# Two graph layers on one core: attention scores with keys on partitions, their sums by a matrix of ones, and a fixed round of stages on TensorE

## The chip, the cores and the metric

The kernel runs on one core of one Trainium2 chip. The metric is the device time of one execution in microseconds. Three executions of the kernel before gave 3097.95, 3098.14 and 3100.08 us; the median is 3098.14 us.

Engines: TensorE (PE, with its weight loads as a row of their own, PEld), VectorE (DVE), ScalarE (ACT), GpSimd (POOL) and SyncE (SP, which issues DMAs here). Matmuls write PSUM, which has eight banks of 2 KB per partition; GpSimd works on SBUF only here. All data is float32.

## The reference

`x` has 64 graphs of 256 nodes with 512 features; `adj` is one 256x256 matrix of zeros and ones, the same for all graphs, symmetric, with ones on its diagonal. Layer 0 is masked attention with 8 heads of 64, a residual and a layer norm; layer 1 is a graph attention layer with one score per pair of nodes, a residual and a layer norm.

```python
q, k, v = x @ Wq + bq, x @ Wk + bk, x @ Wv + bv          # split in 8 heads of 64
scores = q k^T / 8 + (1 - adj) * -1e9
attn = softmax(scores)                                    # over the keys
x = layernorm(x + (attn v) @ Wo + bo)
h = x @ W
s1, s2 = h @ a[:512], h @ a[512:]
e = leaky_relu(s1[:, None] + s2[None, :], 0.2) * adj
x = layernorm(x + elu(softmax(e) h + beta * h))
```

## The kernel before

One graph is called a batch here (b = 0 to 63). Tiles have 128 partitions: a batch's 256 nodes are two blocks t, its 512 features four blocks c.

**A batch's stages.** `tr_x` (line 423) transposes x on TensorE into `xT`, and GpSimd adds the folded biases `res_sb` onto x (428). `project` (301) multiplies by a 512x512 weight with seven block products instead of eight (the sums of blocks come from `weight_sums`, once, and from `token_sums`, four GpSimd subtractions per operand, line 292). A product is made of matmuls at line 315 (result with features on partitions: q, k) or 319 (nodes on partitions: v, o, u). Its results are copied out of PSUM by ACT (lines 442, 445) or DVE (542), and further parts are added by DVE (451, 542). In the projection o both are DVE additions onto x (542). Product 6 accumulates onto the bank of product 1 (`ps_chain`), so it has to wait until product 1's copy has been read; the order on TensorE is products 1, 5, 2, 6, 3, 4, 7.

`scores(t, g)` (467): for a block t of 128 queries and four heads, four matmuls (474) with queries on partitions and 256 keys along the free axis; DVE adds the mask and finds the row minimum of the negated scores (481); ACT takes the exponential with that as bias and sums the row (485); DVE inverts the sums (489); GpSimd multiplies the probabilities by them (490). `flip(h)` (495) transposes a head's probabilities on TensorE (501), so that keys are on partitions, and ACT or DVE copies them out (505, 507). `mix(g)` (511) multiplies them with v (519), and DVE copies the result, `oT` (524). The projection o follows, then `norm` (385).

The second layer: two weighted sums over the features on DVE (555), a small transpose (564, "logits" in the change), the leaky score matrix (569 to 582, with GpSimd's product with `adj` in 573), its transpose (591, "attention" in the change), the mixing of x (`spread`, 605), the projection u, the exponential and two DVE additions (625 to 628), `norm`, and the store (631).

**The order of the work.** Nothing is issued directly: each step is given to `Plan.op` (64) with an engine, a duration, what it reads and writes, and, on TensorE, a mode ("rows" for scores, "columns" for mix, else none). `Plan.place` (91) is a list scheduler: at each step it takes, on the engine that can start first, the ready operation with the earliest start, and the oldest in the program among equals; a change of mode on TensorE costs 250 ns in its books. `slots` (181) limits the live tiles by kind: 8 PSUM banks, 10 tiles of 8 KB and so on. The result is one fixed order of instructions for each engine, all 64 batches unrolled; on the chip every engine works through its list in order and waits by semaphores. Small constants are loaded by the GpSimd queue at the start, the weights by ACT's queue, x and the output by SP's.

Of the kernel before, what the change touches and what calls it, by code (L numbers as in the profile page):

```python
# [9 lines left out]
F32 = mybir.dt.float32  # L10
AF = mybir.ActivationFunctionType
# [8 lines left out]
NEG = -1000000000.0  # L20

# [23 lines left out]
class Plan:  # L45
# [6 lines left out]

    LAG = {"PE": 260.0, "DVE": 70.0, "ACT": 70.0, "POOL": 90.0, "SP": 2200.0, "LD": 2200.0}
    SWITCH = 250.0

    def __init__(self, slots):
        self.slots = dict(slots)
        self.ops = []

# [4 lines left out]
    def op(self, engine, ns, fn, reads=(), writes=(), mode=None, claims=()):  # L64
# [24 lines left out]
        self.ops.append((engine, ns, fn, deps, bufs, mode))  # L89

    def place(self):
# [3 lines left out]
        for n, o in enumerate(ops):  # L95
            need[n] = len(o[3])
            for d in o[3]:
                users[d].append(n)
        end = [0.0] * len(ops)
# [9 lines left out]
        while len(order) < len(ops):  # L109
            best = None  # L110
            for e, cand in ready.items():
                pick = None
                for n in cand:
# [15 lines left out]
                    cost = self.SWITCH if e == "PE" and m != mode else 0.0  # L129
                    key = (max(start + cost, now[e] + 60.0), n)  # L130
# [7 lines left out]
            if e == "PE" and m != mode:  # L138
                start += self.SWITCH
                mode = m  # L140
            for b in bufs:
# [27 lines left out]
def gnn_two_layers(ctx: ExitStack, tc: tile.TileContext, x, adj, Wq, bq, Wk, bk, Wv, bv, Wo, bo, W, a, beta, out):  # L169
# [9 lines left out]
    psum = ctx.enter_context(tc.tile_pool(name="psum", bufs=1, space=PSUM))  # L179

    slots = {"x": 4, "full": 10, "p": 6, "half": 15, "xS": 2, "st": 90, "ps": 8}
# [10 lines left out]
    sb_pool, ps_pool = Pool(big), Pool(psum)  # L192
    plan = Plan(slots)
    A = slice(None)
# [10 lines left out]
    def once(shape, name):  # L205
# [3 lines left out]
        return sb(name, shape, name)  # L209
# [13 lines left out]
    def weight(w, name):  # L223
        w_sb = once([C, D], name)
        plan.op("LD", 4500, lambda: nc.scalar.dma_start(w_sb[A], w.rearrange("(c p) f -> p c f", p=P)), [], [w_sb])
        return w_sb

# [19 lines left out]
    bo_sb = on_all(bo, 0, D, "bo_sb")  # L247
# [3 lines left out]
    a_sb = [on_all(a, i * D, D, f"a{i}_sb") for i in range(2)]  # L251

    mask_sb = once([NT, N], "mask_sb")

    def mask():
        nc.vector.tensor_scalar(mask_sb[A], adj_sb, -1.0, 1.0, ALU.mult, ALU.add)
        nc.vector.tensor_scalar(mask_sb[A], mask_sb[A], NEG * HD ** 0.5, None, ALU.mult)

    plan.op("DVE", 900, mask, [], [mask_sb])


# [83 lines left out]
    def residual_bias():  # L345
        acc = ps([D], "ps_b")
# [7 lines left out]
        plan.op("DVE", 690, lambda: nc.vector.tensor_add(res_sb[A], acc[A], bo_sb), [acc], [res_sb])  # L354
# [6 lines left out]
    def second_layer_constants():  # L361
# [4 lines left out]
        for i in range(2):  # L366
            col = st(C, "col")
            for c in range(C):
                junk = sb("half", [D], "junk")
                plan.op("DVE", 780, lambda c=c, i=i, junk=junk, col=col: nc.vector.scalar_tensor_tensor(  # L370
# [296 lines left out]
```

## Time and profile before

| what | number |
|---|---|
| median of three executions | 3098.14 us |
| profiled execution, its own time | 3099.26 us |
| its span, first to last instruction | 3097.50 us |
| granted TensorE clock over the span | 0.994 |
| PE busy | 3033.8 us |
| PE work per batch away from the ends, start of a mix to the start of the next | 46.99 us |
| DVE, ACT, POOL busy in such a stretch of 46.99 us | 34.10, 25.18, 23.30 us |
| scores, mix, spread and all flips of one batch on PE | 3.65, 3.60, 3.45 and 3.50 us |

"Busy" is the time in which an engine has an instruction in execution. The chain of waits is the list of work that ended last, traced back from the last instruction: an engine with nearly all of it sets the time. A group of instructions carries the line of the kernel, the engine, and the tiles by name, as output<-input. PE's pieces in that chain follow each other without overlap, so their lengths can be added.

### The profile page before, as it was taken

To read this page: it belongs to the slowest core of one execution; us is meant where nothing else is said; L and a number is where in the kernel's file an instruction comes from. 1 tells how busy PE (TensorE), PEld (TensorE's weight loads), DVE (VectorE), ACT (ScalarE), POOL (GpSimd) and SP (SyncE) were. 2 spreads that over 40 slices of the span, in tenths; PEclk is the share of its full clock that TensorE was granted. 3 is DMA by queue.
4 is the path that set the end of the run, shared out by engine and by line. 5 is a ranking of instruction groups with operands and counts; after the bars stand their busy time and mean duration, and the time that the engine had idled before them with its cause. 6 is when DMAs were issued, how large, how long until landed. Compare 5 with 4: busy or idle time off the path is not lost.

```text
span 3097.5 us, 56539 instructions
## 1 busy us (share of the span) xinstructions
PE 3033.8 (98%) x20624; PEld 2673.7 (86%) x20624; DVE 2202.2 (71%) x6303; ACT 1614.5 (52%) x4737; POOL 1521.2 (49%) x1756
## 2 busy tenths in 40 slices
PE   8999999999999999999999999999999999999995
PEld 7778898898898888888988888988988889888884
DVE  4678667677677677676686676776776776766865
ACT  3455555455455555555555554554555555555552
POOL 6355445445445455454454454454554554544543
PEclk9999999999999999999999999999999999999998
DMA  3000000000000000000000000000000000000000
GB/s 109 1 28 28 28 15 28 22 22 28 18 25 28 15 28 28 15 28 28 15 28 28 15 28 21 22 28 18 25 28 15 28 28 15 28 28 15 28 15 14
DMA packets 39205, 77.03 MB, mean 25 GB/s; under 512 B 3344, under 2 KB 3344, under 8 KB 38928
## 3 DMA queue, kind: packets, MB, share of 16 engines
q1 hardware_dynamic: 35840, 67.12, 6.0%
q10 hardware_dynamic: 2640, 5.24, 0.5%
q8 instruction: 164, 2.69, 0.4%
q0 software_dynamic: 448, 1.06, 0.1%
q14 instruction: 113, 0.93, 0.1%
HBM read 39.85 MB, written 33.55 MB: 24 GB/s over the span
## 4 chain that ended last, share of the span: by engine, by line
PE 95%; DVE 2%; POOL 1%; issue 1%; ACT 0%; DMA 0%; SPq 0%; POOLq 0%; ACTq 0%; DVEq 0%
PE ps_chain L319 16%; PE ps_chain L315 11%; PE ps_pair L319 11%; PE ps_cross L319 10%; PE ps_cross L315 7%; PE ps_pair L315 7%; PE ps_sc L474 7%; PE ps_y L605 7%; PE ps_pv L519 7%; PE tr_p L501 7%; PE tr_x L423 2%; PE tr_a L591 1%; PE tr_s L564 0%; DMA x<-in_x_dram 0%; DVE junk L555 0%
## 5 line engine op out<-in xcount | busy, mean ns | idle before, releaser
L485 ACT ACTIVATE p<-p,nm 128x256 f32<-128x256 f32 x1024 | 506.3, 496 | 23.7 <-DVE nm L481 16.4
L490 POOL TENSOR_TENSOR p<-p,rc 128x1024 f32<-128x1024 f32 x256 | 484.3, 1892 | 51.6 <-DVE rc L489 50.3
L481 DVE CUSTOM_DVE_ANT_0 p<-ps_sc,mask_sb 128x256 f32<-128x256 f32 x1024 | 386.0, 413 | 4.6 <-PE ps_sc L474 4.6
L292 POOL TENSOR_TENSOR yS<-yT 128x256 f32<-128x256 f32 x128 | 93.7, 732 | 548.7 <-ACT yT L610 543.7
L392 POOL TENSOR_SCALAR rs<-mv 128x1 f32<-128x1 f32 x256 | 78.5, 306 | 565.5 <-DVE mv L389 565.5
L398 ACT ACTIVATE x<-x,nmr,rs 128x512 f32<-128x512 f32 x256 | 208.3, 814 | 248.0 <-DVE nmr L396 248.0
L501 PE MATMUL tr_p<-ident,p 128*128 128x128 f32 x2048 | 247.7, 274 | 6.1 <-POOL p L490 3.0
L474 PE MATMUL ps_sc<-kT,qT 64*128 64x256 f32 x2048 | 240.5, 383 | 1.9 <-DVE oT L524 1.6
L519 PE MATMUL ps_pv<-pT,v 128*64 128x256 f32 x2048 | 237.6, 384 | 4.4 <-DVE pT L507 2.3
L501 PEld LDWEIGHTS tr_p<-ident,p 128*128 128x128 f32 x2048 | 229.3, 142 | 9.3 <-issue 4.0
L396 DVE SCALAR_TENSOR_TENSOR nmr<-mv,rs 128x1 f32<-128x1 f32 x256 | 227.7, 889 | 13.3 <-POOL rs L393 2.3
L605 PE MATMUL ps_y<-attT,x 128*128 128x256 f32 x1024 | 233.7, 381 | 1.6 <-ACT attT L594 1.6
L474 PEld LDWEIGHTS ps_sc<-kT,qT 64*128 64x128 f32 x2048 | 193.3, 187 | 46.8 <-issue 23.4
L573 POOL TENSOR_TENSOR e<-e,adj_sb 128x512 f32<-128x512 f32 x64 | 81.4, 1271 | 293.5 <-DVE rc L489 275.0
L605 PEld LDWEIGHTS ps_y<-attT,x 128*128 128x128 f32 x1024 | 195.4, 191 | 29.7 <-ACT attT L594 2.6
L519 PEld LDWEIGHTS ps_pv<-pT,v 128*64 128x64 f32 x2048 | 141.6, 138 | 82.4 <-DVE x L628 9.7
L451 DVE TENSOR_TENSOR v<-ps_pair,v 128x256 f32<-128x256 f32 x64 | 27.2, 425 | 232.8 <-PE ps_pair L319 232.8
L485 ACT ACTIVATION_READ_ACCUMULATOR p<-p,nm 128x1 f32 x1024 | 192.1, 188 | 0.0
L388 DVE BATCH_NORM_STATS2 bn<-x 128x6 f32<-128x512 f32 x256 | 175.6, 686 | 6.6
L505 ACT COPY pT<-tr_p 128x512 f32<-128x512 f32 x256 | 148.8, 582 | 51.9 <-PE tr_p L501 45.5
L507 DVE COPY pT<-tr_p 128x512 f32<-128x512 f32 x256 | 169.8, 683 | 5.4 <-PE tr_p L501 5.3
L445 ACT ACTIVATE qT<-ps_chain,bq_sb 128x128 f32<-128x128 f32 x256 | 79.7, 361 | 180.0 <-PE ps_chain L315 180.0
(168 smaller groups left out, 7516.1 us busy)
## 6 DMA issues: line engine op xcount, KB each, us to landing
x<-in_x_dram SPq DMA_DIRECT2D x64, 512.0 KB, 3.6
out_dram<-x SPq DMA_DIRECT2D x128, 256.0 KB, 2.0
wq_sb<-in_L_gnn_Wq_dram ACTq DMA_DIRECT2D x1, 1024.0 KB, 10.0
wk_sb<-in_L_gnn_Wk_dram ACTq DMA_DIRECT2D x1, 1024.0 KB, 7.6
wv_sb<-in_L_gnn_Wv_dram ACTq DMA_DIRECT2D x1, 1024.0 KB, 5.8
wo_sb<-in_L_gnn_Wo_dram ACTq DMA_DIRECT2D x1, 1024.0 KB, 5.5
w_sb<-in_L_gnn_W_dram ACTq DMA_DIRECT2D x1, 1024.0 KB, 5.6
a_sb<-in_L_gnn_a_dram POOLq DMA_DIRECT2D x2, 256.0 KB, 8.5
```

The source lines that it names most:

```text
L315: nc.tensor.matmul(dst[:, f, :], l[:, c, blk(f)], r[:, c, :], start=start and f == 0 and c == 0, stop=c == 1, skip_group_check=True)
L319: nc.tensor.matmul(dst, r[:, c, :], l[:, c, :], start=start and c == 0, stop=c == 1, skip_group_check=True)
L388: plan.op("DVE", 690, lambda: nc.vector.bn_stats(bn[A], X[:, t, :]), [(X, (t, 0)), (X, (t, 1))], [bn])
L396: plan.op("DVE", 150, lambda: nc.vector.scalar_tensor_tensor(nm[A], mv[:, 0:1], -1.0, rs[A], op0=ALU.mult, op1=ALU.mult), [mv, rs], [nm])
L398: plan.op("ACT", 810, lambda: nc.scalar.activation(X[:, t, :], X[:, t, :], AF.Identity, bias=nm[A], scale=rs[A]), [nm, rs], [(X, (t, 0)), ...
L474: nc.tensor.matmul(acc[i % 2][:, i // 2, :], qT[r:r + HD, h // 2, blk(t)], kT[r:r + HD, h // 2, :], start=True, stop=True)
L481: plan.op("DVE", 420, lambda i=i: nc.vector.tensor_tensor_reduce(p[:, i, :], acc[i % 2][:, i // 2, :], mask_sb[:, t, :], -1.0 / HD ** 0.5, ...
L485: plan.op("ACT", 690, lambda i=i: nc.scalar.activation(p[:, i, :], p[:, i, :], AF.Exp, bias=nm[t][g][:, i:i + 1], scale=-1.0, accum_out=sm ...
L490: plan.op("POOL", 1900, lambda: nc.gpsimd.tensor_tensor(p[A], p[A], rc[A].unsqueeze(2).to_broadcast([P, 4, N]), ALU.mult), [rc, p], [p])
L501: nc.tensor.transpose(tr[:, k, blk(t)], pr[t][h // 4][:, h % 4, blk(k)], ident)
L519: nc.tensor.matmul(acc[s * HD:(s + 1) * HD, i, :], V[:, k, h * HD:(h + 1) * HD], pT[h][:, k, :], start=k == 0, stop=k == NT - 1)
L605: nc.tensor.matmul(acc[:, i, :], X[:, j, c * P:(c + 1) * P], attT[:, j, :], start=j == 0, stop=j == NT - 1)
```

## The change

In the first layer the scores are computed with keys on partitions: `kT` is the stationary operand and `qT` the moving one, one PSUM bank per head. ACT takes the exponential straight from PSUM with no maximum subtracted; DVE multiplies it by the transposed `adj` (made once on TensorE); the result is already what mix needs, so the flips and their copies are gone. GpSimd adds a head's two key blocks, and a matmul with a matrix of ones and zeros (`ones`, 32 columns, four results at partitions 0, 32, 64 and 96) sums over the partitions. DVE inverts the sums, SP writes one row per head to DRAM and reads it back onto 64 partitions each (`everywhere`), and DVE multiplies mix's result by it in place of the plain copy. ACT also sums the denominators and their inverses into `range_sb`.

TensorE's order is no longer the scheduler's choice: each TensorE step has a turn, made of a round and a place in `ROUND`. A round holds mix of batch r-1, scores of r, x of r+1, spread of r-2, o of r-1, u of r-2, v of r, logits of r-1, sums of r, q and k of r+1, attention of r-1. On the other engines, among operations that can start equally early, the one needed first by TensorE goes first. The slots change (x 5, tiles of 8 KB 9, of 2 KB 24).

At the end a test of `range_sb` decides whether a general version (maximum subtracted, queries on partitions, a loop over the batches) does all batches again. Two constants now come by ACT's queue when they are needed (`bo`, `a`).

```diff
+    LATER = 20
...
     def place(self):
...
+        turns = [n for _, n in sorted(self.turns, reverse=True)]
+        due = [None] * len(ops)
+        for i, n in enumerate(reversed(turns)):
+            due[n] = i
+        for n in reversed(range(len(ops))):
+            for u in users[n]:
+                if due[u] is not None and (due[n] is None or due[u] < due[n]):
+                    due[n] = due[u]
+        for n, o in enumerate(ops):
+            if due[n] is None:
+                due[n] = max((due[d] + (self.LATER if ops[d][0] == "PE" else 0) for d in o[3]), default=0)
         end = [0.0] * len(ops)
         base = [0.0] * len(ops)
...
                 pick = None
+                if e == "PE":
+                    cand = turns[-1:] if turns and turns[-1] in cand else []
...
                         continue
-                    cost = self.SWITCH if e == "PE" and m != mode else 0.0
-                    key = (max(start + cost, now[e] + 60.0), n)
+                    key = (max(start, now[e] + 60.0), due[n], n)
                     if pick is None or key < pick[0]:
...
             for b in bufs:
                 if not b.held:
...
-    slots = {"x": 4, "full": 10, "p": 6, "half": 15, "xS": 2, "st": 90, "ps": 8}
+    dram = ctx.enter_context(tc.tile_pool(name="dram", bufs=1, space=bass.MemoryType.DRAM))
+    slots = {"x": 5, "full": 9, "half": 24, "xS": 4, "st": 90, "ps": 8, "rows": 4}
...
-    mask_sb = once([NT, N], "mask_sb")
...
-    plan.op("DVE", 900, mask, [], [mask_sb])
+    ones = const.tile([P, 48], F32, name="ones")
+    nc.gpsimd.memset(ones, 0.0)
+    nc.gpsimd.memset(ones[:, 16:32], 1.0)
...
+            for k in range(NT):
+                for t in range(NT):
+                    nc.tensor.transpose(acc[:, k, blk(t)], adj_sb[:, t, blk(k)], ident)
+        plan.op("PE", 430, pe, [], [acc], claims=[adjT_sb])
+        plan.op("DVE", 690, lambda: nc.vector.tensor_copy(adjT_sb[A], acc[A]), [acc], [adjT_sb])
...
+        def turn(what):
+            later = {"x": -1, "q": -1, "k": -1, "scores": 0, "v": 0, "sums": 0, "mix": 1, "o": 1, "logits": 1,
+                     "attention": 1, "spread": 2, "u": 2}[what]
+            plan.turn = (n + later, ROUND.index(what))
+        plan.op("SP", 60, lambda: nc.sync.dma_start(X[A], x[at].rearrange("o (t p) d -> p (o t) d", p=P)), [],
                 [(X, (t, i)) for t in range(NT) for i in range(2)])
-        return X
...
-            acc = [ps([2, N], "ps_sc") for _ in range(2)]
-            def pe():
-                for i in range(4):
-                    h, r = 4 * g + i, (i % 2) * HD
-                    nc.tensor.matmul(acc[i % 2][:, i // 2, :], qT[r:r + HD, h // 2, blk(t)],
-                                     kT[r:r + HD, h // 2, :], start=True, stop=True)
-            plan.op("PE", 870, pe, [(qT, (g, t)), (kT, (g, 0)), (kT, (g, 1))], acc, mode="rows",
-                    claims=[pr[t][g], nm[t][g], sm[t][g]])
-            p = pr[t][g]
-            for i in range(4):
-                plan.op("DVE", 420, lambda i=i: nc.vector.tensor_tensor_reduce(
-                    p[:, i, :], acc[i % 2][:, i // 2, :], mask_sb[:, t, :], -1.0 / HD ** 0.5, 3.0e38, ALU.add,
-                    ALU.min, nm[t][g][:, i:i + 1]), [acc[i % 2], mask_sb], [(p, i), nm[t][g]])
-            for i in range(4):
-                plan.op("ACT", 690, lambda i=i: nc.scalar.activation(
-                    p[:, i, :], p[:, i, :], AF.Exp, bias=nm[t][g][:, i:i + 1], scale=-1.0,
-                    accum_out=sm[t][g][:, i:i + 1]), [(p, i), nm[t][g]], [(p, i), (sm[t][g], i)])
...
-            plan.op("POOL", 1900, lambda: nc.gpsimd.tensor_tensor(
-                p[A], p[A], rc[A].unsqueeze(2).to_broadcast([P, 4, N]), ALU.mult), [rc, p], [p])
...
-            plan.op("PE", 430, pe, [pr[t][h // 4] for t in range(NT)], [tr], claims=[pT[h]])
-            if h % 2:
-                plan.op("ACT", 580, lambda: nc.scalar.copy(pT[h][A], tr[A]), [tr], [pT[h]])
-            else:
-                plan.op("DVE", 690, lambda: nc.vector.tensor_copy(pT[h][A], tr[A]), [tr], [pT[h]])
...
+        def mixed(pT, g, onto, reads=()):
+            turn("mix")
...
-            plan.op("PE", 1740, pe, [(V, (g, 0)), (V, (g, 1))] + pT[4 * g:4 * g + 4], [acc], mode="columns",
-                    claims=[oT])
-            plan.op("DVE", 690, lambda: nc.vector.tensor_copy(oT[:, 2 * g:2 * g + 2, :], acc[A]), [acc], [(oT, g)])
+            plan.op("PE", 1740, pe, [(V, (g, 0)), (V, (g, 1))] + pT[4 * g:4 * g + 4] + list(reads), [acc],
+                    mode="columns", claims=[oT])
+            plan.op("DVE", 690, lambda: onto(acc), [acc] + list(reads), [(oT, g)])
+        def attention_by_keys():
+            pT = [sb("half", [NT, N], "pT") for h in range(H)]
+            both = [sb("half", [2, N], "both") for c in range(C)]
+            inv, everywhere = sb("half", [N], "inv"), sb("full", [C, N], "inv_all")
+            rows = Buf(dram_pool, "rows", [H, N], "rows")
+            def scores(g):
+                turn("scores")
+                acc = [ps([NT, N], "ps_sc") for _ in range(4)]
+                def pe():
+                    for i in range(0, 4, 2):
+                        for k in range(NT):
+                            for s in range(2):
+                                h, r = 4 * g + i + s, s * HD
+                                nc.tensor.matmul(acc[i + s][:, k, :], kT[r:r + HD, h // 2, blk(k)],
+                                                 qT[r:r + HD, h // 2, :], start=True, stop=True)
+                plan.op("PE", 1740, pe, [(m, (g, j)) for m in (qT, kT) for j in range(NT)], acc, mode="rows",
+                        claims=pT[4 * g:4 * g + 4] + both[2 * g:2 * g + 2])
+                for i in range(4):
+                    h = 4 * g + i
+                    plan.op("ACT", 620, lambda h=h, i=i: nc.scalar.activation(
+                        pT[h][A], acc[i][A], AF.Exp, scale=1.0 / HD ** 0.5), [acc[i]], [pT[h]])
+                    plan.op("DVE", 620, lambda h=h: nc.vector.tensor_mul(pT[h][A], pT[h][A], adjT_sb[A]),
+                            [pT[h], adjT_sb], [pT[h]])
+                    plan.op("POOL", 700, lambda h=h: nc.gpsimd.tensor_tensor(
+                        both[h // 2][:, h % 2, :], pT[h][:, 0, :], pT[h][:, 1, :], ALU.add),
+                        [pT[h]], [(both[h // 2], h % 2)])
+            def denominators():
+                turn("sums")
+                acc = ps([N], "ps_den")
+                def pe():
+                    for s in range(2):
+                        for c in range(C):
+                            nc.tensor.matmul(acc[32 * c:32 * c + 32, :], ones[:, 16 - 16 * s:48 - 16 * s],
+                                             both[c][:, s, :], start=s == 0, stop=s == 1)
+                plan.op("PE", 1000, pe, both, [acc], mode="sums", claims=[inv])
+                plan.op("DVE", 2150, lambda: nc.vector.reciprocal(inv[A], acc[A]), [acc], [inv])
+                for i, m in enumerate((acc, inv)):
+                    junk = sb("half", [N], "junk")
+                    plan.op("ACT", 600, lambda i=i, m=m, junk=junk: nc.scalar.activation(
+                        junk[A], m[A], AF.Identity, accum_out=range_sb[:, i, b:b + 1]), [m],
+                        [junk, (range_sb, (i, b))])
+                plan.op("SP", 60, lambda: nc.sync.dma_start(rows[A], inv[0:P:P // H, :]), [inv], [rows])
+                for s in range(2):
+                    def spread(s=s):
+                        r = rows[A]
+                        nc.sync.dma_start(everywhere[s * HD:(s + 1) * HD], bass.AP(
+                            tensor=r.tensor, offset=r.offset + s * N, ap=[[0, HD], [2 * N, C], [1, N]]))
+                    plan.op("SP", 1000, spread, [rows], [(everywhere, s)])
+            def mix(g):
+                mixed(pT, g, lambda acc: nc.vector.tensor_mul(
+                    oT[:, 2 * g:2 * g + 2, :], acc[A], everywhere[:, 2 * g:2 * g + 2, :]), [everywhere])
+            scores(0)
+            scores(1)
+            val()
+            denominators()
+            mix(0)
+            mix(1)
...
+        if general:
+            attention_by_queries()
+        else:
+            attention_by_keys()
...
+    plan.turn = (-1, 0)
+    transposed_mask()
     for b in range(B):
-        batch(b)
+        batch(b, slice(b, b + 1))
...
+    plan.turn = (B + 1, 0)
+    fine, row, least = st(1, "fine"), ps([P], "row"), st(1, "least")
+    ok = sb("half", [2, B], "ok")
+    def check():
+        nc.vector.tensor_scalar(ok[A], range_sb[A], SAFE, None, ALU.is_le)
+        nc.vector.tensor_reduce(fine[A], ok[A], AX.XY, ALU.min)
+    plan.op("DVE", 500, check, [range_sb], [ok, fine])
+    plan.op("PE", 110, lambda: nc.tensor.transpose(row[A], fine[A].to_broadcast([P, P]), ident), [fine], [row],
+            claims=[least])
...
+    again = nc.values_load(bad, skip_runtime_bounds_check_because="a comparison gives 0 or 1")
+    with tc.If(again != 0):
+        mask_sb = sb_pool.tile([P, NT, N], F32, tag="half", name="mask_sb")
+        nc.vector.tensor_scalar(mask_sb, adj_sb, -1.0, 1.0, ALU.mult, ALU.add)
+        nc.vector.tensor_scalar(mask_sb, mask_sb, NEG * HD ** 0.5, None, ALU.mult)
+        with tc.For_i(0, B, 1) as i:
+            for tile_ in stay:
+                tile_.parts = {}
+            plan = Plan({**slots, "half": slots["half"] - 1})
+            batch(None, bass.ds(i, 1), general=True)
```

## The prediction

> **What bounds the kernel now.** I read the page's busy times first, then the chain of waits.
>
> ```profile
> PE 3033.8 (98%) x20624; PEld 2673.7 (86%) x20624; DVE 2202.2 (71%) x6303; ACT 1614.5 (52%) x4737; POOL 1521.2 (49%) x1756
> PE 95%; DVE 2%; POOL 1%; issue 1%; ACT 0%; DMA 0%; SPq 0%; POOLq 0%; ACTq 0%; DVEq 0%
> ```
>
> TensorE is busy for 98% of the span and holds 95% of the chain: only what it executes, or waits for, counts. The chain in order of time (start, length, work) shows one period:
>
> ```profile
> 1505.50 3.60 PE ps_pv L519 x32
> 1509.10 3.65 PE ps_sc L474 x32
> 1512.76 1.06 PE ps_chain L319 x4
> 1513.82 0.86 PE ps_cross L319 x4
> ...
> 1520.78 1.75 PE tr_p L501 x16
> ...
> 1532.59 1.75 PE tr_p L501 x16
> ...
> 1536.80 3.45 PE ps_y L605 x16
> ...
> 1551.61 0.87 PE tr_x L423 x8
> 1552.49 3.60 PE ps_pv L519 x32
> ```
>
> From mix to mix it is 46.99 us without a gap; such periods repeat to the end. The table of windows (length, then busy time and instructions of PE, PEld, DVE, ACT, POOL, then granted clock, DMA share, GB/s) gives head, period and drain:
>
> ```profile
> 0.00:100.00 100.00, 82.96 (x590) 74.85 (x591) 48.32 (x139) 41.78 (x132) 59.79 (x59) 1.00 0.26 85
> 1505.50:1552.49 46.99, 46.98 (x324) 41.62 (x326) 34.10 (x99) 25.18 (x75) 23.30 (x27) 1.00 0.06 23
> 3009.40:3097.50 88.10, 55.67 (x285) 42.24 (x284) 50.66 (x142) 28.16 (x70) 30.52 (x42) 0.83 0.05 18
> ```
>
> 64 periods are 3007 us; the rest, some 90 us, is lost at the two ends, where PE idles 17 and 32 us and, in the drain, runs at a clock of 0.83.
>
> **The change, part by part.** *Scores, mix:* as many half-array matmuls of the same size; nothing. *Flips out:* two pieces of 1.75, so -3.50 us per batch, all on the chain.
>
> *Sums in:* 8 matmuls, 16 instructions in the trace's count, of 256 columns. One alone costs 3.45/16 = 0.216 us (`ps_y`). Two half arrays run at a time (mix: 32 in 3.60). No row shows quarter arrays: four at a time 4 x 0.216 = 0.86, two 1.73, one 3.45. I take four, since the halves overlap fully. A change of mode costs 0.15 in mix (3.60 - 16 x 0.216) and 0.20 in the first piece after scores (1.06 against 0.86); sums adds two: +0.35. So +1.21, between 1.21 and 3.80.
> The Trainium skill (TensorE: Matmul & The Clock Gate, Part 3) measured 3.07x for four row tiles; by that the sums take 3.45/3.07 = 1.12 + 0.35, and my sum grows by 17 us.
>
> *Round on PE:* 46.99 - 3.50 + 1.21 = 44.70 if nothing waits. Counted from mix: mix to 3.60, scores to 7.25, x to 8.32, spread to 11.77, o to 17.8, u and v (6.04 each) to 29.9, logits 30.1, sums 31.3, q and k (6.25 each) 43.9, attention 44.6.
>
> *ACT:* loses lines 485 and 505 (506.3, 192.1, 148.8 us, 13.2 per batch), gains 8 exponentials at 0.62 (line 625, the same size) and two range sums at about 0.56: 18 us of 45. *DVE:* loses 481, 489, 507 (10.6 per batch), gains 8 products at 0.68 and a reciprocal of 256; 4 elements took 0.164 and 2 took 0.155, so 1.3 us by that slope; the plan books 2.15. About 31 us. *POOL:* loses 7.6 (line 490), gains 8 additions at 0.735: about 22 us. None becomes the bound by its sum.
>
> *Sums to mix by DRAM:* reciprocal at most 2.15, a store 2.0 (as the output's), a read 3.6 (as x's, also 512 KB): 7.8 us. q, k, attention and the first half of mix, 15 us, hide it. On SP these DMAs wait for the reciprocal and for each other, with the stores of r-2 and the next load of x behind them; x has five tiles and a round to spare, so nothing follows. Without that cover each microsecond costs 62.
>
> *The new wait, DVE against POOL.* The groups look harmless, but where both read SBUF, DVE instructions with two SBUF inputs stretch. DVE, then POOL:
>
> ```profile
> 154.92 0.68 DVE L555 SCALAR_TENSOR_TENSOR junk<-x,wa_sb 128x512 f32<-128x512 f32 x1
> 155.53 1.20 DVE L555 SCALAR_TENSOR_TENSOR junk<-x,wa_sb 128x512 f32<-128x512 f32 x1
> 156.66 1.20 DVE L555 SCALAR_TENSOR_TENSOR junk<-x,wa_sb 128x512 f32<-128x512 f32 x1
> ```
>
> ```profile
> 155.18 1.00 POOL L292 TENSOR_TENSOR yS<-yT 128x256 f32<-128x256 f32 x1 [1.41 <-ACT yT L610]
> 156.26 1.05 POOL L292 TENSOR_TENSOR yT<-yT 128x256 f32<-128x256 f32 x1
> 157.39 1.05 POOL L292 TENSOR_TENSOR yS<-yT 128x256 f32<-128x256 f32 x1
> ```
>
> Alone they take 0.68 and 0.73; together each pair takes 1.13. Line 481, with one input in PSUM, kept 0.41 beside POOL. The new product has both inputs in SBUF, POOL's addition has the same 256 columns, and they alternate head by head, after four `oS` subtractions. Worked from the round's clock: first exponential done 5.55 (half a group of scores at 4.66, 0.27 to be seen, 0.62); POOL in its second subtraction until 6.13; eight products at 1.13, the last done 14.6. The plan books 620 ns each and has them done near 10.5, so behind them in DVE's fixed order stand the copy of `yT` (0.6, done 15.2) and o's first addition (0.4, done 15.65). o's product 6 accumulates onto that bank and is due at 14.36: **PE waits 1.3 us per round**. After it DVE catches up: o to logits has 12.1 us for a chain of 6.3 (drain, 3060.2 to 3066.5), logits to attention 13.7 for 5.7 (3067.0 to 3072.7).
> The Trainium skill (SBUF — State Buffer, Who interferes with whom) speaks against the change: of such a pair the second is blocked for the whole instruction. By it the wait would be 3.4 us and the sum 132 us higher; the rows, with 1.13 per pair, show less.
> From the rows, the wait has as ends 0 (the additions fall in gaps) and 3.4 (each pair in full sequence, 0.68 + 0.73 = 1.41: products done 16.6, o's addition 17.7); I take 1.3, since 1.13 was measured on the same sizes.
>
> *Round:* 44.70 + 1.3 = 46.0.
>
> *Ends.* q starts at 18.9 as now (weights and first clock). Round -1 to 32; bias 3.45, scores, x and v to 46; sums wait for POOL, which first does four weight sums at 1.27, then eight pairs at 1.13, to 50.5; with sums, q and k to 64. Round 1 lacks spread and u and waits about 2 more: to 103. Drain: round 63 without x, q, k, with attention waiting 4.5: 38; round 64: 28; round 65: 11; last norm and store 10.4 (3087.1 to 3097.5); low clock 4 as now.
> *Branch:* the test is done before the last spread. What every engine adds is a register load and a jump; no row shows one. Two short DMA landings (2.0) and a little, 5 us; ends 0 and 15.
> *Constants by ACT, transposed adj:* hidden in the head's wait for x and weights (first `tr_x` 6.6, q 18.9); at most 2 us if late.
>
> *Sum:* 103 + 61 x 46.0 (2806) + 38 + 28 + 11 + 10.4 + 4 + 5 = 3005.4 span, + 1.76 around it (3099.26 - 3097.50) = 3007.2, against 3099.26; the median lies 1.1 below that execution: **3006 us**.
>
> **The rivals.** *A, the collision stays off PE* (DVE's order puts o's additions before the last products): 63 x 1.3 less, **2924**. For it: collisions in the steady periods of before cost PE nothing. Against: there they fell on single-column steps (line 396, mean 889 ns, against 160 free), not on eight in a row.
> *B, quarter arrays run two at a time:* 0.87 x 64 more, **3062**.
> *C, slower: logits come late.* PE now may not go around a late stage; before it put q's products between. With the longest durations seen, o to logits is 0.27 + 0.76 + 0.70 + 0.19 (line 389) + 1.15 (rs) + 1.27 (POOL busy) + 1.85 (line 396) + 0.82 + four times 1.74 (line 370 beside POOL's long additions) = 14.0, against 12.1 of cover; with 0.4 of hand-overs a wait of 2.3 per round: 3006 + 62 x 2.3 = **3149**. It decides from 1.6 us on. For it: the head, where this chain took 13.3 (145.0 to 158.3). Against: there eight of line 481 shared DVE.
> *D, the test fails and all is done twice:* near 6000 us; inputs are normal, scores have a spread near 1.
>
> **How the numbers follow.** A difference of 0.2%, 6 us, is about what a measurement tells from none. Forecast 0.50 (its own range 2970 to 3045: wait 0.8 to 1.9, ends +-10), A 0.24, B 0.10, C 0.12, D 0.01, sums of small waits that end near 3098 0.03. Faster: 0.50 + 0.24 + 0.10 = 0.84; same 0.03; slower 0.13. The range reaches over A and B and leaves out C, D and a tail of A: 2915 to 3100.
>
> **What would show it.** Right: a period near 46.0 with no flips; sums near 0.9 in the chain; line of the product near 1.1 us instead of 0.68; PE's `ps_chain` of o waiting for DVE. A: that wait absent, period 44.7. B: sums 1.7. C: `tr_s` waiting for DVE's line 555. Wrong would also be PE waiting for the DMA onto `everywhere`, or more than 15 us after the last store.

## The result and the profile after

The changed kernel takes 3236.68 us (median of four runs, 3233.88 to 3238.35), against 3098.11 us for the kernel before in the same comparison: a ratio of 1.0445, interval 1.0427 to 1.0463. The forecast was 3006 us, in a range of 2915 to 3100. The profiled execution took 3238.35 us, its span is 3236.5 us.

The page's busy times and its chain of waits, kernel after:

```profile
PE 2947.3 (91%) x19605; PEld 2518.0 (78%) x19605; DVE 2126.2 (66%) x4322; ACT 1267.0 (39%) x3201; POOL 1598.9 (49%) x2011
PE 53%; POOL 35%; issue 7%; DVE 3%; ACT 2%; DMA 0%; POOLq 0%; DVEq 0%
```

TensorE is busy for 86.5 us less than before (3033.8) and the kernel is 139 us longer. Its share of the chain fell from 95% to 53%, and GpSimd, which held 1%, holds 35%. GpSimd is not the bound by its sum: it is busy for 49% of the span, as before. It is late at one place in each round. The waits of TensorE, kernel after (us in total, how often, the longest):

```profile
PE ps_chain L361 <- ACT u L492: 202.2, 61, 3.3
PE ps_chain L361 <- DVE x L675: 43.8, 63, 2.0
PE tr_s L699 <- DVE junk L690: 2.8, 3, 1.9
```

The second is the wait that was forecast, in o. The first, 202.2/61 = 3.31 us per round in u, was not. The chain in order of time, one round of the kernel after:

```profile
1500.73 3.63 PE ps_pv L526 x32
...
1512.32 2.37 POOL both L560 x3
...
1523.23 2.49 POOL x L476 x2
1525.71 0.20 POOL rs L435
1525.99 0.58 POOL rs L436
1526.59 0.17 DVE nmr L439
1526.78 0.81 ACT x L441
1527.59 0.27 ACT u L492
1527.90 1.99 PE ps_chain L361 x8
...
1535.30 1.00 PE ps_den L572 x16
...
1549.44 3.63 PE ps_pv L526 x32
```

It reads as follows. Mix starts at 1500.73. GpSimd's additions (L560) are slow. Behind them in its list stand subtractions for x and u, the last addition, and both additions of the biases onto x (L476, 2.49 us). Only then come the two instructions for the norm's `rs`, at 1525.7. The norm on ACT (L441) needs them, and it stands ahead of a copy of u. This is the timeline of ACT, kernel after (start, length, line, work, and in brackets the idle time and what ended it):

```profile
1521.17 0.37 ACT L492 COPY u<-ps_cross 128x256 f32<-128x256 f32 x1 [0.49 <-PE ps_cross L361]
1526.78 0.81 ACT L441 ACTIVATE x<-x,nmr,rs 128x512 f32<-128x512 f32 x1 [5.24 <-DVE nmr L439]
1527.50 0.35 ACT L492 COPY u<-ps_chain 128x256 f32<-128x256 f32 x1
```

The matmuls that the last copy reads were issued at 1521.83 and ended at 1522.86. The copy stood ready from then on, behind a norm that waited for GpSimd, and ACT was idle for 5.24 us. u's product 7 accumulates onto that bank:

```profile
1515.71 1.10 PE L361 MATMUL ps_chain<-so_sb,oS 128*128 128x256 f32 x4 [0.65 <-DVE x L675]
1527.90 1.13 PE L361 MATMUL ps_chain<-sw_sb,yS 128*128 128x256 f32 x4 [3.32 <-ACT u L492]
```

(Timeline of PE, kernel after.) So TensorE waits for ACT, ACT for DVE, DVE for GpSimd, and on each the order is fixed, with other work behind the instruction that waits.

The table of windows of the kernel after (columns as in the prediction: length, busy times, clock, DMA share, GB/s) shows two rounds in succession:

```profile
1500.73:1549.44 48.71, 44.74 (x309) 38.48 (x310) 32.80 (x69) 19.77 (x50) 24.61 (x31) 1.00 0.10 33
1549.44:1599.84 50.40, 46.42 (x308) 39.64 (x310) 32.90 (x69) 19.74 (x50) 24.62 (x31) 0.97 0.10 32
```

48.71 - 44.74 = 3.97 us is idle, and 0.65 + 3.32 is 3.97. The second round is 1.7 us longer in TensorE's own time: its clock is 0.97. The mean of rounds 2 to 62 is 49.81 us. All of the error lies here: 61 x (49.81 - 46.0) = 232 us, and the span exceeds the forecast span by 3236.5 - 3005.4 = 231 us.

Where the extra time in the second round comes from shows in four windows of 3.41 us, kernel after, the first two around u's wait in one round, the last two in the next:

```profile
1522.90:1526.31 3.41, 1.69 (x8) 1.14 (x6) 0.00 (x0) 0.00 (x0) 3.33 (x5) 1.00 0.00 0
1526.31:1529.72 3.41, 1.82 (x8) 1.63 (x9) 2.41 (x9) 2.04 (x4) 0.99 (x3) 1.00 0.00 0
1574.10:1577.51 3.41, 0.89 (x4) 0.82 (x5) 1.49 (x5) 2.02 (x4) 1.83 (x5) 1.00 0.00 0
1577.51:1580.92 3.41, 3.41 (x10) 2.69 (x9) 3.38 (x11) 0.40 (x2) 0.00 (x0) 0.50 0.02 5
```

The same wait of 3.3 us fell on two windows in the first round and mostly on one in the second, and there the next window ran at a clock of 0.50. More on this in the last section.

### The profile page after: what moved, and what is told of

Read it like the earlier page. It is cut to its first block, busy times and chain, and to the rows that moved or that the text cites. A ratio compares the mean times of both kernels' runs of the same rounds, so it can differ in the third digit from the quotient of the medians.

```text
span 3236.5 us, 51666 instructions
## 1 busy us (share of the span) xinstructions
PE 2947.3 (91%) x19605; PEld 2518.0 (78%) x19605; DVE 2126.2 (66%) x4322; ACT 1267.0 (39%) x3201; POOL 1598.9 (49%) x2011
## 4 chain that ended last, share of the span: by engine, by line
PE 53%; POOL 35%; issue 7%; DVE 3%; ACT 2%; DMA 0%; POOLq 0%; DVEq 0%
POOL both L560 12%; PE ps_chain L357 11%; PE ps_chain L361 9%; PE ps_pv L526 7%; PE ps_cross L357 7%; PE ps_pair L357 7%; POOL oS L334 5%; POOL x L476 5%; PE ps_cross L361 4%; POOL yS L334 4%; PE ps_pair L361 4%; POOL xS L334 3%; PE ps_den L572 2%; ACT x L441 2%; POOL yT L334 1%
## 5 line engine op out<-in xcount | busy, mean ns | idle before, releaser
L558 DVE TENSOR_TENSOR pT<-pT,adjT_sb 128x512 f32<-128x512 f32 x512 | 555.1, 1141 | 61.9 <-ACT pT L556 61.9
L560 POOL TENSOR_TENSOR both<-pT 128x256 f32<-128x256 f32 x512 | 531.7, 1067 | 4.6 <-DVE pT L558 4.6
L556 ACT ACTIVATE pT<-ps_sc 128x512 f32<-128x512 f32 x512 | 257.6, 627 | 259.8 <-PE ps_sc L549 259.8
L441 ACT ACTIVATE x<-x,nmr,rs 128x512 f32<-128x512 f32 x256 | 207.9, 812 | 379.2 <-DVE nmr L439 379.2
L361 PE MATMUL ps_chain<-sw_sb,yS 128*128 128x256 f32 x512 | 148.5, 415 | 202.2 <-ACT u L492 202.2
L439 DVE SCALAR_TENSOR_TENSOR nmr<-mv,rs 128x1 f32<-128x1 f32 x256 | 41.2, 161 | 306.3 <-POOL rs L436 303.4
L549 PE MATMUL ps_sc<-qT,kT 64*128 64x256 f32 x2048 | 238.4, 382 | 0.0
L549 PEld LDWEIGHTS ps_sc<-qT,kT 64*128 64x128 f32 x2048 | 192.8, 187 | 44.7 <-issue 24.8
L690 DVE SCALAR_TENSOR_TENSOR junk<-x,wa_sb 128x512 f32<-128x512 f32 x256 | 163.4, 693 | 3.0
L476 POOL TENSOR_TENSOR x<-x,res_sb 128x512 f32<-128x512 f32 x128 | 159.5, 1267 | 0.0
L436 POOL TENSOR_TENSOR rs<-rs,neg_half 128x1 f32<-128x1 f32 x256 | 144.2, 563 | 21.3
```

Of the source, the lines that this page charges most:

```text
L361: nc.tensor.matmul(dst, r[:, c, :], l[:, c, :], start=start and c == 0, stop=c == 1, skip_group_check=True)
L441: plan.op("ACT", 810, lambda: nc.scalar.activation(X[:, t, :], X[:, t, :], AF.Identity, bias=nm[A], scale=rs[A]), [nm, rs], [(X, (t, 0)), ...
L476: plan.op("POOL", 1270, lambda: nc.gpsimd.tensor_tensor(X[:, t, :], X[:, t, :], res_sb[A], ALU.add), [res_sb], tokens(t))
L549: nc.tensor.matmul(acc[i + s][:, k, :], kT[r:r + HD, h // 2, blk(k)], qT[r:r + HD, h // 2, :], start=True, stop=True)
L556: plan.op("ACT", 620, lambda h=h, i=i: nc.scalar.activation(pT[h][A], acc[i][A], AF.Exp, scale=1.0 / HD ** 0.5), [acc[i]], [pT[h]])
L558: plan.op("DVE", 620, lambda h=h: nc.vector.tensor_mul(pT[h][A], pT[h][A], adjT_sb[A]), [pT[h], adjT_sb], [pT[h]])
```

## The experiments

Times are medians; ratios are to the kernel before, run beside each.

**1. No additions on GpSimd.** The matmuls of the sums, 16 instead of 8, read `pT` itself.

```diff
-                    plan.op("POOL", 700, lambda h=h: nc.gpsimd.tensor_tensor(
-                        both[h // 2][:, h % 2, :], pT[h][:, 0, :], pT[h][:, 1, :], ALU.add),
-                        [pT[h]], [(both[h // 2], h % 2)])
...
+                        for k in range(NT):
+                            for c in range(C):
+                                nc.tensor.matmul(acc[32 * c:32 * c + 32, :], ones[:, 16 - 16 * s:48 - 16 * s],
+                                                 pT[2 * c + s][:, k, :], start=s == 0 and k == 0,
+                                                 stop=s == 1 and k == NT - 1)
```

> Edit: GpSimd's eight additions per batch go; the matmuls with ones read both key blocks of each head instead, 16 matmuls in place of 8. Same results. Theory (DVE's products and GpSimd's additions hold each other up, GpSimd then comes late with the layer norm, and u's copy on ACT stands behind that norm): products back from 1.14 us to about 0.7 apart from the few that meet the oS subtractions, no PE wait in u, at most 0.3 in o; period 44.7 + 0.87 for the longer sums = 45.6 to 45.9; time 2975 to 2995. Rival (the fixed round itself makes PE wait, whatever DVE and GpSimd do): the 3.3 us wait in u stays, 3270 to 3300.

Measured 3067.15 us, ratio 0.9892 (0.9875 to 0.9908), round 47.08. A miss, between the two theories' ranges: the wait in u is gone, but o's grew to 109.1/62 = 1.76 us. The groups of this kernel say why:

```profile
L557 DVE TENSOR_TENSOR pT<-pT,adjT_sb 128x512 f32<-128x512 f32 x512 | 617.2, 1263 | 61.9 <-ACT pT L555 61.9
L476 POOL TENSOR_TENSOR x<-x,res_sb 128x512 f32<-128x512 f32 x128 | 215.3, 1702 | 0.0
```

The products did not get faster (1263 ns): with the additions gone, the additions of the biases, 1.27 us alone and 1.70 here, ran in that stretch and collided in their place. The collision was moved, not removed.

**2. True durations in the plan.** The collision stays, but the list scheduler is told of it.

```diff
-                    plan.op("DVE", 620, lambda h=h: nc.vector.tensor_mul(pT[h][A], pT[h][A], adjT_sb[A]),
+                    plan.op("DVE", 1130, lambda h=h: nc.vector.tensor_mul(pT[h][A], pT[h][A], adjT_sb[A]),
-                    plan.op("POOL", 700, lambda h=h: nc.gpsimd.tensor_tensor(
+                    plan.op("POOL", 1130, lambda h=h: nc.gpsimd.tensor_tensor(
```

> Edit: the plan books 1130 ns instead of 620 for the product and instead of 700 for the addition; nothing else. The collision stays. Theory: products and additions still take about 1.1 us each, but now the plan knows, puts GpSimd's rs ahead of the addition of the bias onto x and u's third copy ahead of the norm on ACT; PE's wait in u falls from 3.3 to under 0.5, the one in o stays near 0.7 or falls; period 45.0 to 45.8, time 2945 to 2990. Rival (the two engines are overloaded in this stretch and order does not help): the wait only moves, to o or to logits, and the time stays above 3150.

Measured 3048.47 us, ratio 0.9834 (0.9817 to 0.985), round 46.72: again between the two theories' ranges. Products and additions still take 1107 and 950 ns, but 3.1 us of the round are gone, from the order alone; 1.1 of them are the clock, which is not halved in any steady round. What is left, waits of PE:

```profile
PE ps_chain L361 <- ACT v L492: 77.7, 61, 1.3
PE ps_chain L357 <- ACT qT L495: 44.2, 61, 0.7
```

The new order also brought a second collision, seen in this kernel's groups. The additions of the biases, now behind `rs`, run beside the weighted sums for logits. In the kernel after the sums take 693 ns and these additions 1267; here both stretch:

```profile
L690 DVE SCALAR_TENSOR_TENSOR junk<-x,wa_sb 128x512 f32<-128x512 f32 x256 | 316.9, 1289 | 0.1
L476 POOL TENSOR_TENSOR x<-x,res_sb 128x512 f32<-128x512 f32 x128 | 215.0, 1699 | 0.0
```

**3. The norm booked 4.5 us later** in layer 0, so that the plan puts u's copies ahead of it on ACT.

```diff
                 if not need[u]:
+                    base[u] += self.late.get(u, 0.0)
...
-            norm(X, t)
+            norm(X, t, 4500)
```

> Edit: in the plan alone, ACT's step of the first layer's norm counts as ready 4.5 us later, so that it stands behind u's copies on ACT; GpSimd's and TensorE's order and all durations stay. Theory (PE waits in u only because u's copy is queued on ACT behind a norm that waits for GpSimd): the 3.3 us wait goes, products still 1.14 us, the wait of 0.65 in o stays; period 45.4 to 45.9, time 2970 to 2995. Rival (GpSimd's lateness reaches PE on another way, by logits): PE's small transpose tr_s then waits 2 to 3 us for DVE's line of the weighted sums; time above 3100.

Measured 3104.57 us, ratio 1.0016 (1.0007 to 1.0026), round 47.48: in the rival's range, though logits wait 47.7/65 = 0.73 us, not 2 to 3. The wait in u is gone, so the place was right, but the late norm shows up again at two others, the first two here; the third is o's wait, as before the edit. Waits of PE:

```profile
PE ps_chain L363 <- ACT v L495: 77.4, 61, 1.6
PE tr_s L702 <- DVE junk L693: 47.7, 65, 4.1
PE ps_chain L363 <- DVE x L678: 43.8, 63, 2.1
```

The middle one is the wait of rival C: logits come late once the norm is put back further. Order around the late norm recovers 2.3 us of a round. The norm now starts 29.3 us after mix instead of 26.1, so part of the new waits comes from the edit itself; this run can't separate them.

**4. No mask product at all.** All nodes attend to all.

```diff
-                    plan.op("DVE", 620, lambda h=h: nc.vector.tensor_mul(pT[h][A], pT[h][A], adjT_sb[A]),
-                            [pT[h], adjT_sb], [pT[h]])
```

> Edit: DVE's product with the transposed adj is left out, so all nodes attend to all; the rest stays, additions on GpSimd too. Theory: without a partner the additions take 0.73 us, GpSimd's norm is on time, no wait in u or o; period 44.7 to 44.9, span 2920 to 2935. Rival (GpSimd's own list is too long or too badly ordered, the partner does not matter): additions drop to 0.73 but the bias addition of 2.5 us still stands before rs, a wait of 1 us or more in u stays; span 2990 or more.

A single execution: 2966.16 us, span 2964.4, round 45.41, between the two theories' numbers. Additions fall to 730 ns and o's wait goes, but u's stays at 55.8/61 = 0.91 us. So the product beside the additions is most of the loss, the order of the work (biases ahead of `rs`, the norm ahead of u's copy) the rest.

**5. Products in turns.** u's and v's products alternate on TensorE, and q's and k's, so that four products lie between a copy's matmuls and product 7's need of it, not two.

```diff
+            plan.turn = turn + ((1, 5, 2, 6, 3, 4, 7).index(n),)
...
-            plan.turn = (n + later, ROUND.index(what))
+            place = ROUND.index({"v": "u", "k": "q"}.get(what, what))
+            plan.turn = (n + later, place)
```

> Edit: the changed kernel with the fixed order on TensorE altered in one thing: the seven products of u and of v take turns (u1, v1, u5, v5, ...), and so do those of q and k. The product that accumulates onto a bank then stands behind four other products (3.45 us of TensorE time, four times 0.86) instead of two (1.73). The collision of the mask product with GpSimd's additions is left as it is. Theory (the mask products make GpSimd's list late, the norm waits for it, and the norm stands ahead of u's copy on ScalarE, for which product 7 of u waits 3.3 us per round): 1.7 us of that wait is covered by the longer gap, and what is left is too short for the clock to be halved; o's wait of 0.65 stays. Round 49.8 - 1.7 - 0.9 = 47.2 us if the order elsewhere stays, down to 45.5 where the copies of v move ahead of the norm too: 3000 to 3090 us. Rival (GpSimd and VectorE have too little time in a round for the whole of their lists, wherever TensorE waits): the wait turns up at another place with the same 3 to 4 us, and the time stays at 3200 us or above.

Measured 3138.39 us, ratio 1.0129 (1.0112 to 1.0146), round 47.97 at full clock, 48.14 on the mean: outside both theories' ranges. The wait for ACT's copy of u is gone, and two others, together smaller, came. Waits of PE:

```profile
PE ps_pair L361 <- DVE u L505: 98.6, 61, 1.8
PE ps_cross L361 <- ACT v L496: 44.4, 61, 0.7
PE ps_chain L361 <- DVE x L679: 43.6, 63, 2.1
```

The norm starts as late as before (26.12 us after mix in both kernels, median of the rounds). Now a copy of v stands behind it on ACT, and on DVE an addition of u stands behind the four weighted sums for logits, which need the norm.

**6. The collision itself: the transposed adj stays in PSUM.** The product then has one input in SBUF. The price is one bank: seven are left for the rest.

```diff
-    slots = {"x": 5, "full": 9, "half": 24, "xS": 4, "st": 90, "ps": 8, "rows": 4}
+    slots = {"x": 5, "full": 9, "half": 24, "xS": 4, "st": 90, "ps": 7, "rows": 4}
...
-    adjT_sb = once([NT, N], "adjT_sb")
+    slots["adjT"] = 1
+    plan.slots["adjT"] = 1
+    adjT_sb = Buf(ps_pool, "adjT", [P, NT, N], "adjT")
...
-        plan.op("DVE", 690, lambda: nc.vector.tensor_copy(adjT_sb[A], acc[A]), [acc], [adjT_sb])
```

> Edit: the changed kernel with the transposed adj left in the PSUM bank in which TensorE makes it (seven banks for the rest instead of eight), so that the mask product on VectorE has one input in SBUF and one in PSUM, and not two in SBUF. Nothing is left out. Theory (two SBUF inputs collide with GpSimd's additions): the product takes 0.62 to 0.75 us instead of 1.14, the addition 0.73 instead of 1.07, o's wait goes, GpSimd reaches the variance of the norm about 2.4 us earlier, and the wait of u's product 7 falls from 3.3 to about 0.9 us as where the product was left out. Round 45 to 46 us, time 2940 to 3000 us; up to 0.5 us more per round if seven banks hold TensorE back at a copy. Rival one (the pair is slow because both engines are in use, not by the operands): product and addition stay above 1.0 us and the time at 3200 us or above. Rival two (the order on GpSimd and ScalarE makes the wait, not the collision): product and addition get shorter, but u's wait stays at 2 us or above, and the time at 3080 us or above.

Measured 2967.36 us, ratio 0.9573 (0.9557 to 0.9589), round 45.50, as the theory expected. Groups of this kernel, then of the kernel after:

```profile
L561 POOL TENSOR_TENSOR both<-pT 128x256 f32<-128x256 f32 x512 | 355.3, 734 | 3.2 <-DVE pT L559 3.1
L559 DVE TENSOR_TENSOR pT<-pT,adjT 128x512 f32<-128x512 f32 x512 | 312.0, 680 | 61.9 <-ACT pT L557 61.9
```

```profile
L558 DVE TENSOR_TENSOR pT<-pT,adjT_sb 128x512 f32<-128x512 f32 x512 | 555.1, 1141 | 61.9 <-ACT pT L556 61.9
L560 POOL TENSOR_TENSOR both<-pT 128x256 f32<-128x256 f32 x512 | 531.7, 1067 | 4.6 <-DVE pT L558 4.6
```

Same instruction, same size, same neighbour: 680 ns against 1141. The norm starts 22.75 us after mix, 3.4 us earlier. The round is nearly as short as without the product at all (45.41): the product itself was not the cost, its second operand's place was. One wait is left, `ps_pair` of u for DVE, 63.5/61 = 1.04 us.

**7. The same with durations booked as they are** (690 and 750 ns).

> Edit: the kernel with the transposed adj in PSUM, whose plan now books 690 and 750 ns for mask product and addition, as they are (before 620 and 700). Products are not put in turns. It tells which part of the step from 2967 to 2917 us came from the turns. Theory (the wait of 1.03 us in u is the short gap between a copy and product 7, behind nmr on VectorE; bookings that are off by 0.05 us change little): the order stays nearly as it is, round 45.2 to 45.6 us, time 2945 to 2975 us. Rival (the bookings were what mattered): 44.6 to 44.9 us, time 2915 to 2935 us.

Measured 2957.86 us, ratio 0.9541 (0.9525 to 0.9557), round 45.33, as the theory expected; what is left is again the copy of u behind the norm, 51.1/61 = 0.84 us. Bookings are worth 0.17 us of a round here.

**8. Number 7 with the products in turns.**

> Edit: the two edits together (products of u with v and of q with k in turns; transposed adj left in its PSUM bank), and the plan books 690 and 750 ns for mask product and addition, instead of 620 and 700. Theory: both parts of the cause are gone, the collision and the short gap between a copy and the product that needs it; TensorE's work per round is 44.7 us, waits below 0.6 us. Round 44.8 to 45.4 us, time 2925 to 2970 us. Rival (what is left is set by VectorE's or GpSimd's total work): the round stays at 46 us or above, the time at 3000 us or above.

Measured 2916.93 us, ratio 0.9411 (0.9395 to 0.9427), a little below the expected range: round 44.57, TensorE's own work, so the turns are worth the last 0.76 us. No wait of the steady rounds is left, and TensorE holds the chain again:

```profile
PE 2863.4 (98%) x19605; PEld 2477.6 (85%) x19605; DVE 1904.7 (65%) x4321; ACT 1258.3 (43%) x3201; POOL 1407.4 (48%) x2011
PE 96%; POOL 1%; DVE 1%; issue 0%; DMA 0%; ACT 0%; POOLq 0%
```

This version is faster than both kernels.

**9. Turns and true durations, collision left in.**

> Edit: products of u with v and of q with k in turns, as in the first of these kernels, and the plan books 1130 ns for mask product and addition instead of 620 and 700; the collision itself stays. Theory: with true durations alone the round was 46.7 us, with 1.28 us of wait for a copy of v behind the norm and 0.7 us for a copy of q; the longer gap (1.7 us more) covers both, and the round is 44.8 to 45.5 us, time 2925 to 2975 us. Rival (the collision makes VectorE late by itself, whatever the order): o waits for VectorE as in the changed kernel or longer, the round is 46 us or above, the time 3000 us or above.

Measured 3099.46 us, ratio 1.0003 (0.9993 to 1.0012), where 2925 to 2975 was expected: the clearest miss. Rounds are 46.39, or 48.07 where a window at half clock falls into them. PE's one steady wait is for DVE's `v`, 115.4/61 = 1.89 us. The timelines of DVE and of POOL in this kernel:

```profile
1555.44 1.08 DVE L694 SCALAR_TENSOR_TENSOR junk<-x,wa_sb 128x512 f32<-128x512 f32 x1
1556.45 1.74 DVE L694 SCALAR_TENSOR_TENSOR junk<-x,wa_sb 128x512 f32<-128x512 f32 x1
1558.12 1.74 DVE L694 SCALAR_TENSOR_TENSOR junk<-x,wa_sb 128x512 f32<-128x512 f32 x1
1560.75 0.41 DVE L505 TENSOR_TENSOR v<-ps_pair,v 128x256 f32<-128x256 f32 x1
```

```profile
1555.93 3.38 POOL L480 TENSOR_TENSOR x<-x,res_sb 128x512 f32<-128x512 f32 x2
```

The plan moved the additions of the biases behind `rs`, and there they met the weighted sums, which have two inputs in SBUF as well: 1.74 us instead of 0.69. With the products in turns, an addition of v that product 4 of v waits for stands behind them on DVE. The expectation counted one collision; experiment 2 had already shown the second.

**10. The lateness without the collision.** Three more additions on GpSimd ahead of the biases in kernel 6.

```diff
+            def bias():
+                for _ in range(0 if t else 3):
+                    nc.gpsimd.tensor_tensor(spare, spare, spare, ALU.add)
+                nc.gpsimd.tensor_tensor(X[:, t, :], X[:, t, :], res_sb[A], ALU.add)
```

> Edit: the kernel with the transposed adj in PSUM (no collision, round 45.50 us) with three more additions of 128x512 on GpSimd, on a spare tile, ahead of each batch's first addition of the biases, not known to the plan: the lateness of GpSimd is put back without the collision. Theory (the collision costs time by making GpSimd's list late, and in no other way): rs comes 3.7 us later (three by 1.24 us), the wait in u grows from 1.03 to 4.5 - 4.8 us, the round is 49.2 us, and where the clock is halved as in the changed kernel 50.3 on the mean: time 3190 to 3270 us, product and addition still 0.68 and 0.73 us. Rival (a late GpSimd is harmless, it is VectorE held up that costs): time below 3020 us.

Measured 3315.96 us, ratio 1.0693 (1.0675 to 1.0711). Product and addition stay at 681 and 732 ns, `rs` comes 3.2 us later, and the wait in u grows by as much. Waits of PE:

```profile
PE ps_pair L364 <- DVE u L509: 259.0, 61, 4.3
```

259.0/61 = 4.25 against 1.04. The time is above the expected range, with a round of 51.20: 45.50 + 3.2 is 48.7, and the other 2.5 us are clock, halved for 6.8 us in every round.

**11. The collision without some of the lateness.** In the changed kernel, with its order, the additions of the biases touch one column.

```diff
-            plan.op("POOL", 1270, lambda: nc.gpsimd.tensor_tensor(X[:, t, :], X[:, t, :], res_sb[A], ALU.add),
+            plan.op("POOL", 1270, lambda: nc.gpsimd.tensor_tensor(X[:, t, 0:1], X[:, t, 0:1], res_sb[:, 0:1], ALU.add),
```

> Edit: the changed kernel, with its order on every engine, but GpSimd's addition of the biases onto x does 1 column of 512 (left out: the biases in the other columns). The collision of the mask product stays. Theory (the norm comes late because GpSimd's list reaches the two instructions for rs late, and the product 7 of u waits behind the norm on ScalarE): the two additions take 2.5 us of that list ahead of rs, so rs and the norm come 2.2 to 2.4 us earlier, u's wait falls from 3.3 to 0.9 - 1.1, the clock is no longer halved in the middle (mean of a round 49.8, without half clock 48.7), and the round is 46.3 to 46.5 us: time 3015 to 3040 us. Rival (the wait in u is set by VectorE or by the copies on ScalarE, not by GpSimd): u's wait stays at 2.5 us or above, and the time above 3120 us.

Measured 3039.55 us, ratio 0.9802 (0.9786 to 0.9818), round 46.54, in the theory's range, at its upper end. The product still takes 1142 ns. `rs` comes 2.16 us earlier and u's wait falls by 2.16:

```profile
PE ps_chain L361 <- ACT u L492: 70.2, 61, 1.2
PE ps_chain L361 <- DVE x L675: 43.9, 63, 2.1
```

The clock is not halved in any steady round. Numbers 10 and 11 together show the path: TensorE's wait in u moves one to one with the time at which GpSimd reaches `rs`, whatever made it late.

## Why the prediction was wrong, point by point

- **TensorE's work** (44.70 us): 44.74 measured in the window above, 44.57 where nothing waits (experiment 8). Flips out held. Sums in: predicted 0.86 + 0.35 = 1.21; the piece takes 1.00 and the first piece of q behind it 0.20 more than its fellows, 1.20. Rival B, two at a time, is out.
- **The collision**, 1.13 us per pair: 1.141 and 1.067. The sizing, from the weighted sums beside GpSimd's subtractions in the head of the kernel before, was right to 1% for the product and 6% too high for the addition.
- **o's wait**, "PE waits 1.3 us per round": 0.65. The plan put the copy of `yT` ahead of the eighth product, which then ran without a partner (0.67 us), so o's first addition was done 14.84 us after mix, not 15.65. Rival A, no wait, is out too.
- **The step that failed** is the sentence behind it, "After it DVE catches up: o to logits has 12.1 us for a chain of 6.3", and with it the round's only term for waits, 1.3 us in o: a wait in u was put at nothing. A chain of 6.3 was read in the drain, where GpSimd has little else to do. In the round shown it took 10.7 (1519.44 to 1530.16), most of the difference while `mv` was ready at 1521.14 and `rs` started at 1525.68: 4.54 us in GpSimd's list. The collision slows both of a pair, and the prediction followed it down DVE's list only. GpSimd's had the longer tail, eight additions at 1.07 instead of 0.73, then the biases. Without the collision (experiment 6) the norm comes 3.4 us earlier: eight additions of 0.33 less are 2.7, and oS's subtractions, which meet the products too (885 and 1053 ns against 729 and 733), make 0.6.
- **Where it landed.** Logits still came in time, since 10.7 is inside the 12.1 of cover. Rival C had "1.27 (POOL busy)" ahead of `rs`, but carried it on to logits alone, and that wait came to 2.8 us in the whole run. What is queued behind the norm on ACT was not listed: the copy of u, for which product 7 waits 3.32 us. Rival C had the sign, not the mechanism.
- **The clock** in the middle was taken as 1.00, as in the steady periods of before: there, nothing waited. With a wait of 3.3 us it costs 49.81 - 48.71 = 1.1 us per round, 67 us in all, which is nearly half of the distance to the kernel before.
- **The round**, term by term: 44.74 + 0.65 + 3.32 + 1.10 = 49.81.
- **The ends** held: round 2 starts at 103.9 (103), round 63 takes 38.2 (38), from the last mix to the end 56.2 us (58.4 by the sum). The last is partly luck. The branch cost about 0.8 us, from the last norm's end to the end of the span 4.0 against 3.2 before; 5 was taken, and the rest of that stretch was taken 2 us too short.
- **Sums to mix by DRAM** stayed hidden: the read landed in 3.7 us (3.6 taken), the reciprocal took 1.75 (1.3 to 2.15).

What rests on argument: that rounds of 48.7 us would have remained without the clock is read from the rounds in which it was not halved; no run kept the wait and fixed the clock. Why the collision takes 1.14 us, and not the full sequence of 1.41, is open.

## What to carry to other kernels

When two instructions slow each other, follow both engines' lists to the end of the round, and write down for each instruction that will be late what stands behind it in its engine's fixed order, on every engine that it releases in turn. A scheduler that books a duration which neighbours can stretch writes an order that is wrong in just that place: repairing the order recovered part (experiments 2, 3 and 5) and moved a collision to other instructions (1, 2 and 9), while taking away the cause, one operand left in PSUM, recovered 4.3 us of a round at once. Widening the gap between a copy and the matmul that needs it depends on what else is late: it gained 98 us on the changed kernel (5), lost 51 on top of the true durations (9 against 2), and gained 41 with the collision gone (8 against 7).

## What the runs showed of the hardware

- **Which operands collide.** A DVE product of 128x512 takes 0.680 us beside GpSimd's additions with one input in PSUM and 1.141 with both in SBUF; the additions 0.734 and 1.067. The Trainium skill (SBUF — State Buffer, Who interferes with whom) says the same of the operands: one SBUF input does not contend, two do. By its full blocking a pair would take, as an estimate, 0.68 + 0.73 = 1.41; the runs show 1.14.
- **The clock follows windows on a fixed grid.** All half-clock stretches away from the ends of a run start at a multiple of 3.413 us from each other and last one or two such windows. In the four windows shown above, a wait of 3.3 us split evenly over two of them (1.72 and 1.59 us idle) left the clock alone, and the same wait with 2.52 us in one window halved the next. Over the kernel after, windows at full clock that stood ahead of a half one had 1.96 us or more of idle, the others up to 1.95. Other kernels draw the line elsewhere: in experiment 9, windows with 1.87 to 1.90 us came out both ways; in experiment 5, 1.74 us did it and 1.84 once did not; in experiment 1, 1.76 us never did it; and near the start of the kernel before, 1.36 us did it once. So the line lies near half a window, idle time alone does not settle it, and the phase of a wait counts as much as its length. The Trainium skill (TensorE: Matmul & The Clock Gate, Part 1) gives one idle window of about 3.4 us as the condition; the runs show that less than 2 us in one window can do.
- **Rounds can lock to that grid.** In experiment 10 every round is 51.20 us, which is 15 x 3.413. In the kernel after two rounds make 48.71 + 50.40 = 99.11, 0.12 more than 29 x 3.413; windows at half clock follow each other at 29 windows, and about every twelve rounds, when the drift has added up, a further one comes and a round takes 51.5. In experiment 5, whose round is 47.97, they did not lock: the wait drifts over the grid, and only about every tenth round is 1.7 us longer.
- **Four matmuls with 32 columns each run at once:** 16 instructions of 256 columns take 1.00 us, where 16 with a whole array take 3.45.
